# Accumulating attention scores of successive key tiles in one PSUM bank per head, instead of starting a bank for every key tile

## The chip, the cores and the metric

The kernel runs on one core of a Trainium2 chip. The metric is the device time of one execution in microseconds. The engines are named as in the profile: PE (TensorE's matmuls), PEld (its weight loads), DVE (VectorE), ACT (ScalarE), POOL (GpSimd), SP (SyncE, which issues the transfers). Matmul results land in PSUM, which has eight banks of 128 partitions by 512 fp32 values.

## The reference

A transformer layer of attention and a mixture of experts, both fed with the same normalised input; everything is fp32. Attention has 4 sequences of 2048 tokens, width 512, 16 heads of 32.

```python
xn = _layernorm(x, axis=-1)
# attention
qkv = jnp.einsum('bnc,dc->bnd', xn, qkv_w) + qkv_b
q, k, v = ...
attn = jnp.einsum('bhqd,bhkd->bhqk', q, k) * HEAD_DIM ** (-0.5)
attn = jax.nn.softmax(attn, axis=-1)
out = jnp.einsum('bhqk,bhkd->bhqd', attn, v)
a = jnp.einsum('bnc,dc->bnd', out, proj_w) + proj_b
# experts: the first token of a sequence chooses two of eight for the whole sequence
_, idx = jax.lax.top_k(xn[:, 0, :] @ Wr + br, 2)
h = jax.nn.gelu(jnp.einsum('bsd,bkde->bkse', xn, W1[idx]) + b1[idx], approximate=False)
o = jnp.einsum('bkse,bkef->bksf', h, W2[idx]) + b2[idx]
return x + a + jnp.sum(o, axis=1) / 2
```

## The kernel before

**Units.** Attention is cut into 1024 units. The order is: 4 sequences, 4 groups of 4 heads (GH = 4, 32 rows of the array for each head), 4 chunks of 512 queries (CH), 16 tiles of 128 keys (NT). The number of a unit is U, its key tile kt. The loop over U starts 22 units early (LEAD), since each unit also does the first pass of the unit that lies 22 ahead: the maxima of the scores. A chunk's softmax is computed in two passes. The first pass (`score_max`, L526) computes scores with queries on the partitions, 128 queries by 512 keys per head, and DVE reduces each bank to a column of negated maxima (L662). At the end of a chunk the maxima are split into three bf16 parts (`split`), transposed (`turn_maxima`) and kept as `negm`.

**The second pass of a unit**, with keys on the partitions: `shift` (L536) starts a bank for each of the 4 heads with minus the maximum of every query, a bf16 matmul of `ones_b` and `negm`; `score` (L544) adds the scores of 128 keys by 512 queries onto it; ACT takes the exponential from the bank into the tile `p` (L656, 4 instructions a unit, one per head). `weigh` (L556) multiplies p with v in every even unit, for the two units before, into one bank `acc`, which DVE adds to `sacc` (L565, or L562 for the first of a chunk). POOL adds the p of a chunk up to `psum` (L573, L575), one addition of 128x2048 for each key tile but the first; `add_keys` (L581) sums those over the keys.

**The order in a unit** is written out by hand (`manual_schedule`): the four shifts, then scores of heads 0 and 1, maxima of heads 2 and 3, scores of heads 2 and 3, maxima of heads 0 and 1 (so that four matmuls use the four row groups at once); then the exps, a Gelu where one is due, the four reduces, reciprocals and the attention's division, POOL's addition, in even units `weigh`, and last, in most odd units, one item of other work: a projection to q, k or v, a quarter of an expert layer or of the output projection (`dense`, L395, tiles kps, qps, vps, hps, ops, prps), 16 matmuls of 128x32 tiles. Its bank is emptied by DVE or ACT. A planner (`Plan`) places these items in the odd units; 38 odd units remain without one, most of them at kt = 13.

**PSUM.** All of it is one pool of 8 banks taken in turn (`ps`, bufs=8), by `s`, `m`, `acc`, the projections, transposes and key sums alike. A bank's new tile waits for the engine that read the old one. A unit with an `acc` or a projection takes nine banks: s0 to s3, m2, m3, m0, m1, then the ninth.

**SBUF.** `p` has 4 buffers of 8 KB a partition. `kT` holds the keys of a group as 4 tiles of 512 (2 groups at a time), `qT` the queries.

Of the kernel before, what the change touches and what calls it, by code (L numbers as in the profile page):

```python
# [9 lines left out]
F32 = mybir.dt.float32  # L10
BF16 = mybir.dt.bfloat16
U32 = mybir.dt.uint32
AF = mybir.ActivationFunctionType
ALU = mybir.AluOpType
# [3 lines left out]
P = 128  # L18
HEADS = 16
HD = 32  # L20
GH = P // HD
TOP_K = 2
EPS = 1e-5
CH = 512


AHEAD = 6
WARN = 4


class Plan:
# [6 lines left out]
    def __init__(self, B, DC, NCH, NT, TPC):  # L38
        self.per_group = NCH * NT
        self.per_seq = DC * self.per_group  # L40
        self.units = B * self.per_seq
        self.lead = NT + AHEAD
        self.items = {}
# [43 lines left out]
        for b in range(B):  # L87
            t0 = slots[0] if b == 0 else self.first_load[("xf", (b, 0))] + WARN
            for c in range(NCH):
# [4 lines left out]
        for b in range(B):  # L94
            for qc in range(NCH):
# [3 lines left out]
                self.first_load[("xl", ("at", b, qc))] = done + 1  # L99
                proj.append((done + 1 + WARN, [("proj", b, qc, i) for i in range(TPC)]))  # L100

# [64 lines left out]
    def loads(self, bufs, start):  # L166
# [3 lines left out]
        for s, tag, key in self.uses:  # L170
            tiles = live.setdefault(tag, [])
            if key not in [t[0] for t in tiles]:
                free = start
                if len(tiles) == bufs[tag]:
                    free = tiles.pop(0)[1]
                at = max(free, s - 2 * WARN, start, self.first_load.get((tag, key), start))
                assert at < s, (s, tag, key, at, free)
# [9 lines left out]
def block_kernel(  # L187
# [16 lines left out]
    nc = tc.nc  # L204
    B, N, D = x.shape
    E = Wr.shape[1]
    DC = D // P
    NT = N // P
    NCH = N // CH
    TPC = CH // P  # L210
    SCALE = float(HD) ** -0.5
    PSUM = bass.MemoryType.PSUM
    plan = Plan(B, DC, NCH, NT, TPC)
# [2 lines left out]
    ctx.enter_context(tc.manual_schedule())  # L216
    const = ctx.enter_context(tc.tile_pool(name="const", bufs=1))
    kv_pool = ctx.enter_context(tc.tile_pool(name="kv", bufs=2 * NCH))
    p_pool = ctx.enter_context(tc.tile_pool(name="p", bufs=4))
    pair = ctx.enter_context(tc.tile_pool(name="pair", bufs=2))  # L220
    stream = ctx.enter_context(tc.tile_pool(name="stream", bufs=1))
    small = ctx.enter_context(tc.tile_pool(name="small", bufs=2))
    ps = ctx.enter_context(tc.tile_pool(name="ps", bufs=8, space=PSUM))

    def bank(name):
        return ps.tile([P, CH], F32, tag="bank", name=name)

    def rows_of(j):
        return slice(j * HD, (j + 1) * HD)


    xn_dram, v_dram, att_dram, part_dram = {}, {}, {}, {}
# [70 lines left out]
    ones_b = const.tile([P, P], BF16, name="ones_b")  # L303
# [4 lines left out]
    for i in range(2):  # L308
        t = const.tile([P, TPC, GH, HD], BF16, name=f"spread{i}")
# [6 lines left out]
    for c, tag in enumerate(("xl", "xf", "h", "h")):  # L316
        t = stream.tile([P, TPC, D], F32, tag=tag, name=f"x_0_{c}", bufs=2 if tag == "h" else 1)
# [79 lines left out]
                    start=(first and n == 0), stop=(last and n == len(terms) - 1),  # L397
                )

    kT, qT = {}, {}  # L400
    hT, bias, b1s = {}, {}, {}

    def with_bias(dst, src, col, on_dve):
# [102 lines left out]
    def place(u):  # L506
        rest, kt = divmod(u, NT)
        rest, qc = divmod(rest, NCH)
        return (*divmod(rest, DC), qc, kt)

    mx, negm, sacc, psums, sums, pT = {}, {}, {}, {}, {}, {}
    curves, waiting, ends = {}, {}, []

    def later(u, do):
        waiting.setdefault(u, []).append(do)
# [12 lines left out]
            )  # L528
            tiles.append((mx[b, g, qc][:, j, i, kc : kc + 1], t))

    def shift(u, heads, tiles):
        b, g, qc, kt = place(u)
        for j in heads:
            tiles[j] = bank(f"s{j}_{u}")
            r = rows_of(j)
            nc.tensor.matmul(  # L536
                tiles[j], ones_b[r, :], negm[b, g, qc][r, :], start=True, stop=False
            )

    def score(u, heads, tiles):  # L540
        b, g, qc, kt = place(u)
        for j in heads:
            r = rows_of(j)
            nc.tensor.matmul(  # L544
                tiles[j], kT[b, g, kt // TPC][r, ts(kt % TPC, P)], qT[b, g, qc][r, :],
                start=False, stop=True,
            )

    def weigh(u):

# [74 lines left out]
    def divide(where):  # L625
        att[where] = pair.tile([P, CH], F32, tag="att", name="att_%d_%d_%d" % where)
        nc.gpsimd.tensor_tensor(att[where], sacc[where], sums[where], ALU.mult)
# [8 lines left out]
    for U in range(-LEAD, plan.units):  # L636
        second = U >= 0
        first_pass = U + LEAD if U + LEAD < plan.units else None
        chunk, kt = divmod(U, NT)
        b, g, qc, _ = place(U) if second else (0, 0, 0, 0)  # L640
        maxima, tiles = [], {}


        if second:
            shift(U, range(GH), tiles)
        for h in range(2):
            if second:
                score(U, (2 * h, 2 * h + 1), tiles)
            if first_pass is not None:
                score_max(first_pass, (2 - 2 * h, 3 - 2 * h), maxima)  # L650


        if second:
            pT[U] = p_pool.tile([P, GH, CH], F32, tag="p", name=f"p_{U}")
            for j in range(GH):
                nc.scalar.activation(pT[U][:, j, :], tiles[j], AF.Exp, scale=SCALE)  # L656
        curve = curves.pop(U, None)
        if curve is not None:
            flat = curve.rearrange("p f n -> p (f n)")
            nc.scalar.activation(flat, flat, AF.Gelu)  # L660
        for dst, t in maxima:
            nc.vector.tensor_reduce(dst, t, AX.X, ALU.max, negate=True)  # L662
        last = U + LEAD
        if first_pass is not None and last % NT == NT - 1:
            where, n = place(last)[:3], last // NT
            rest = split(where, n)
            mark = U
            pending = (rest, where, n, mark)
        if last % NT == 0 and 0 < last <= plan.units:
            pending[0]()  # L670
        before = place(U - NT)[:3] if U >= NT else None
        if before is not None and kt in (5, 7, 9, 11):
            q = ts((kt - 5) // 2, P)
            nc.vector.reciprocal(sums[before][:, q], sums[before][:, q])  # L674
        if before is not None and kt == 12:
            divide(before)
            later(U + 2, lambda w=before: nc.sync.dma_start(
                att_dram[w[0], w[2]][:, w[1], :], att[w]))
        for t, key in row_ready.pop(U, []):
            nc.gpsimd.tensor_tensor(t, t, bias[key[0]], ALU.add)  # L680
        if second:
            add_weights(U)


        if second and U % 2 == 0:
            if U >= 2:
                weigh(U - 2)
            if U - 2 >= plan.units - NT:
                add_last(U - 2)
            if kt == 4 and before is not None:  # L690
                add_keys(before, bank("keys_%d_%d_%d" % before), [psums[before]], False)
        for step, sb, n in plan.extra.get(U, []):
            if step == "stats":
                if n == 0:
                    norms[sb] = stat_tiles(sb)
                stats(norms[sb][0], n, held["xl", ("stats", sb, n // TPC)][:, n % TPC, :])
            elif step == "root":
                root(*norms[sb], 0, NT)
            elif step == "normal":
                normal(held["xl", ("normal", sb, n // TPC)][:, n % TPC, :], *norms[sb][1:], n)  # L700
            else:
                c, i = divmod(n, TPC)
                xs = held["xq", ("stage", sb, c)]
                turn(xs, held["xl", ("normal", sb, c)][:, i, :], i, f"{sb}_{n}")
                if i == TPC - 1:
                    later(U + 1, lambda sb=sb, c=c, xs=xs: nc.sync.dma_start(xn_dram[sb, c], xs))
        if last % NT == 3 and NT < last <= plan.units + 3:
            turn_maxima(*pending[1:3])
        for item in plan.items.get(U, []):
            dense(item, U, curve is not None)  # L710


        for do in waiting.pop(U, []):
            do()
        for s, tag, key in loads.get(U, []):
            t = load(tag, key)
            if tag == "row":
                row_ready.setdefault(U + 4, []).append((t, key))
        if g == 2 and qc == 0 and kt == 0 and second and b + 1 < B:
            new_bias = load_bias(b + 1)  # L720
        if g == 2 and qc == 0 and kt == 5 and second and b + 1 < B:
            sum_bias(*new_bias)

        for n, c in ((16, NCH - 1), (1, NCH - 2)):
            if U == plan.units - n:
                tags = ("xf", "xq") if c == NCH - 1 else ("xl", "xq")
                t, rows = (
                    stream.tile([P, TPC, D], F32, tag=tag, name=f"end_{tag}", bufs=BUFS[tag])
                    for tag in tags
                )  # L730
                for i in range(TPC):
                    nc.sync.dma_start(rows[:, i, :], part_dram[B - 1, c, i])
                n = DC - 1 if c == NCH - 1 else DC
                nc.sync.dma_start(t[:, :n, :], att_dram[B - 1, c][:, :n, :])
                ends += [t, rows]


    U = plan.units
    weigh(U - 2)
    add_last(U - 2)  # L740
    where = place(U - 1)[:3]
# [69 lines left out]
```

## Time and profile before

| | |
|---|---|
| median of 3 runs | 5135.53 us (5134.29 to 5135.7) |
| the profiled execution | 5133.48 us, its span 5131.6 us |
| TensorE's granted clock | 0.998 |
| first shift, last shift | 160.1 us, 5085.2 us |
| L662, 4096 maxima on DVE | 2542.9 us busy, 683 ns each |
| L656, 4096 exps on ACT | 2118.1 us busy, 602 ns each |
| L544, 4096 scores, and L526, 4096 maxima, on PE | 1924.0 and 1908.4 us busy, side by side |
| L395, six kinds of projections on PE | 1806 us busy in all |

An fp32 matmul is two records in the profile, one for each pass over the moving operand; 8192 records are 4096 matmuls. The matmuls of the four row groups (or column groups) run side by side, so the busy time of a group is the union of its records and a record's mean length is not what it adds. The matmul's own ends are modelled; the intervals between starts are the better measure. The line "idle before, releaser" says how long an engine stood still just before a group's instructions and who let it go on. In the timeline the columns are start, length, engine, line, operation, tiles, and the idle time before it.

### The profile page before, as it was taken

The numbers are of one execution on the slowest core, as the hardware profiler recorded it, in microseconds if no ns is written. First come the engines' busy times: TensorE is split into PE (matmuls) and PEld (weight loads), VectorE is DVE, ScalarE is ACT, GpSimd is POOL, SyncE is SP. The second block draws the span as 40 slices with busy tenths as digits, with TensorE's granted clock in tenths as the row PEclk, the third lists the DMA queues.
The fourth block names the chain that finished last, engine by engine and source line by source line (L and its number), as shares of the span: only waits on it lengthen the run. The fifth ranks groups of instructions, "written<-read, shape, count | busy, mean of one in ns | idle before, by whom it ended". The sixth has DMA issues, their size and how long they took to land.

```text
span 5131.6 us, 108175 instructions
## 1 busy us (share of the span) xinstructions
PE 5054.0 (98%) x46020; PEld 1776.4 (35%) x46020; DVE 3449.0 (67%) x5495; ACT 2516.2 (49%) x4571; POOL 4534.6 (88%) x1430
## 2 busy tenths in 40 slices
PE   8999999999999999999999999999999999999998
PEld 2333333333333333333333333333333333333333
DVE  5666676766766667666766767766667666666672
ACT  1455545554544545554445454555444454555543
POOL 0699898989999999999999999989999999999992
PEclk9999999999999999999999999999999999999999
DMA  4211112201122112221121221221112211021112
GB/s 165 69 62 51 46 65 89 102 30 38 67 85 69 65 65 80 72 81 44 48 93 46 79 85 54 85 85 59 40 56 89 78 63 59 18 75 34 40 43 78
DMA packets 220675, 340.20 MB, mean 66 GB/s; under 512 B 14364, under 2 KB 129052, under 8 KB 205984
## 3 DMA queue, kind: packets, MB, share of 16 engines
q1 hardware_dynamic: 220192, 333.28, 19.2%
q8 instruction: 361, 5.91, 0.5%
q14 instruction: 122, 1.00, 0.1%
HBM read 249.61 MB, written 83.62 MB: 65 GB/s over the span
## 4 chain that ended last, share of the span: by engine, by line
PE 95%; POOL 2%; ACT 1%; DVE 0%; issue 0%; DMA 0%; SPq 0%; ACTq 0%; POOLq 0%
PE acc L556 18%; PE m L526 17%; PE s L544 17%; PE ops L395 9%; PE hps L395 9%; PE s L536 7%; PE kps L395 4%; PE vps L395 4%; PE qps L395 4%; PE prps L395 4%; POOL psum L575 2%; PE keys L581 1%; ACT L656 1%; PE xt L365 1%; ACT p L656 1%; PE mt L618 0%
## 5 line engine op out<-in xcount | busy, mean ns | idle before, releaser
L575 POOL TENSOR_TENSOR psum<-psum,p 128x2048 f32<-128x2048 f32 x882 | 4008.6, 4545 | 217.3 <-ACT p L656 182.1
L662 DVE TENSOR_REDUCE mx<-m 128x1 f32<-128x512 f32 x4096 | 2542.9, 683 | 1057.5 <-PE m L526 1056.9
L656 ACT ACTIVATE p<-s 128x512 f32<-128x512 f32 x4096 | 2118.1, 602 | 1797.3 <-PE m L526 1717.9
L544 PE MATMUL s<-qT,kT 32*128 32x512 f32 x8192 | 1924.0, 589 | 0.0
L526 PE MATMUL m<-kT,qT 32*128 32x512 f32 x8192 | 1908.4, 590 | 2.7 <-DMA wk<-in_qkv_wT_dram 1.5
L526 PEld LDWEIGHTS m<-kT,qT 32*128 32x128 f32 x8192 | 929.1, 184 | 325.3 <-issue 242.3
L556 PE MATMUL acc<-p,v 128*32 128x512 f32 x8192 | 990.0, 599 | 38.5 <-ACT p L656 38.5
L544 PEld LDWEIGHTS s<-qT,kT 32*128 32x128 f32 x8192 | 765.6, 186 | 31.0 <-issue 12.8
L556 PEld LDWEIGHTS acc<-p,v 128*32 128x32 f32 x8192 | 215.3, 109 | 738.5 <-ACT p L656 428.6
L395 PE MATMUL hps<-xf,w 128*32 128x512 f32 x4096 | 466.0, 595 | 0.2 <-ACT p L656 0.2
L395 PE MATMUL ops<-wb_w,h 128*32 128x512 f32 x4096 | 466.0, 595 | 0.2 <-ACT p L656 0.2
L536 PE MATMUL s<-negm,ones_b 32*128 32x512 bf16 x4096 | 421.4, 385 | 5.3 <-ACT p L656 3.5
L565 DVE TENSOR_TENSOR sacc<-acc,sacc 128x512 f32<-128x512 f32 x448 | 309.9, 692 | 154.7 <-PE acc L556 154.7
L536 PEld LDWEIGHTS <-ones_b 32*128 32x128 bf16 x4096 | 108.6, 91 | 842.3 <-issue 835.2
L573 POOL TENSOR_TENSOR psum<-p,p 128x2048 f32<-128x2048 f32 x63 | 286.1, 4541 | 117.6 <-ACT p L656 117.6
L407 ACT ACTIVATE h<-hps,b 128x512 f32<-128x512 f32 x115 | 79.0, 687 | 353.6 <-PE hps L395 353.6
L674 DVE RECIPROCAL sums<-sums 128x128 f32<-128x128 f32 x252 | 237.3, 942 | 0.7 <-ACT sums L593 0.7
L395 PE MATMUL vps<-wb_v,xq 128*32 128x512 f32 x2048 | 233.0, 595 | 2.3 <-issue 2.0
L395 PEld LDWEIGHTS ops<-wb_w,h 128*32 128x32 f32 x4096 | 120.0, 109 | 317.6 <-issue 229.8
L395 PEld LDWEIGHTS hps<-xf,w 128*32 128x32 f32 x4096 | 120.0, 109 | 317.1 <-issue 232.1
L395 PE MATMUL kps<-xq,wk 128*32 128x512 f32 x1920 | 218.4, 595 | 1.0 <-ACT p L656 0.2
L395 PE MATMUL qps<-xq,wq 128*32 128x512 f32 x1920 | 218.4, 595 | 0.1
(89 smaller groups left out, 1710.8 us busy)
## 6 DMA issues: line engine op xcount, KB each, us to landing
xq<-xn_dram SPq DMA_DIRECT2D x64, 1024.0 KB, 5.7
w<-in_W_dram SPq DMA_DIRECT2D x128, 256.0 KB, 3.1
xn_dram<-xq_stage SPq DMA_DIRECT2D x16, 1024.0 KB, 7.1
v_dram<-v SPq DMA_DIRECT2D x64, 256.0 KB, 2.4
xf<-xn_dram SPq DMA_DIRECT2D x16, 1024.0 KB, 6.1
v<-v_dram SPq DMA_DIRECT2D x64, 256.0 KB, 4.0
row<-in_x_dram SPq DMA_DIRECT2D x64, 256.0 KB, 5.9
part_dram<-row SPq DMA_DIRECT2D x64, 256.0 KB, 2.1
```

The source lines that it names most:

```text
L395: nc.tensor.matmul(pp[rows_of(j), :], lhsT[:, rows_of(j)], rhs, start=(first and n == 0), stop=(last and n == len(terms) - 1),)
L407: nc.scalar.activation(dst, src, AF.Identity, bias=col)
L526: nc.tensor.matmul(t, qT[b, g, qc][r, ts(i, P)], kT[b, g, kc][r, :], start=True, stop=True)
L536: nc.tensor.matmul(tiles[j], ones_b[r, :], negm[b, g, qc][r, :], start=True, stop=False)
L544: nc.tensor.matmul(tiles[j], kT[b, g, kt // TPC][r, ts(kt % TPC, P)], qT[b, g, qc][r, :], start=False, stop=True,)
L556: nc.tensor.matmul(acc[r, :], held["v", (b, g, kt // TPC)][:, (kt + n) % TPC, r], pT[u + n][:, j, :], start=(n == 0), stop=(n == 1),)
L565: nc.vector.tensor_tensor(t, acc, t, ALU.add)
L573: nc.gpsimd.tensor_tensor(psums[b, g, qc], pT[u - 1], pT[u], ALU.add)
L575: nc.gpsimd.tensor_tensor(psums[b, g, qc], psums[b, g, qc], pT[u], ALU.add)
L656: nc.scalar.activation(pT[U][:, j, :], tiles[j], AF.Exp, scale=SCALE)
L662: nc.vector.tensor_reduce(dst, t, AX.X, ALU.max, negate=True)
L674: nc.vector.reciprocal(sums[before][:, q], sums[before][:, q])
```

## The change

One bank per head (`s_bank`) now belongs to the scores for the whole kernel. The shift is put in once at the start of a chunk. The scores of the first key tile are added onto it, and each following key tile adds q times the *difference* between its keys and those of the tile before (`kD`), so that the bank holds, after each unit, the shifted scores of that unit's keys. The exp reads the bank between two such additions.

- `shift` runs in 64 units instead of 1024.
- `differences` makes `kD` on DVE: for each group and each of its 4 key tiles of 512, one subtraction of 384 columns and, but for the first tile, one of 128. They stand behind the reduces in the units with kt = 7, 11 and 15 before a group and kt = 3 in it.
- The rotating pool `ps` has 4 banks instead of 8, for `m`, `acc`, the projections, transposes and key sums.
- `p` has 3 buffers instead of 4; the room goes to `kD` (4 tiles of 2 KB a partition).

```diff
+DIFF = 55
...
-    p_pool = ctx.enter_context(tc.tile_pool(name="p", bufs=4))
+    p_pool = ctx.enter_context(tc.tile_pool(name="p", bufs=3))
...
-    ps = ctx.enter_context(tc.tile_pool(name="ps", bufs=8, space=PSUM))
+    ps = ctx.enter_context(tc.tile_pool(name="ps", bufs=4, space=PSUM))
+    s_pool = ctx.enter_context(tc.tile_pool(name="s", bufs=1, space=PSUM))
...
+    s_bank = [s_pool.tile([P, CH], F32, tag=f"s{j}", name=f"s{j}") for j in range(GH)]
...
-    def shift(u, heads, tiles):
-        b, g, qc, kt = place(u)
-        for j in heads:
-            tiles[j] = bank(f"s{j}_{u}")
-            r = rows_of(j)
-            nc.tensor.matmul(
-                tiles[j], ones_b[r, :], negm[b, g, qc][r, :], start=True, stop=False
-            )
+    def shift(where):
+        for j in range(GH):
+            r = rows_of(j)
+            nc.tensor.matmul(s_bank[j], ones_b[r, :], negm[where][r, :], start=True, stop=True)
 
-    def score(u, heads, tiles):
+    def score(u, heads):
         b, g, qc, kt = place(u)
+        k = (kD if kt else kT)[b, g, kt // TPC]
         for j in heads:
             r = rows_of(j)
             nc.tensor.matmul(
-                tiles[j], kT[b, g, kt // TPC][r, ts(kt % TPC, P)], qT[b, g, qc][r, :],
-                start=False, stop=True,
+                s_bank[j], k[r, ts(kt % TPC, P)], qT[b, g, qc][r, :],
+                start=False, stop=True, skip_group_check=True,
             )
+
+    def differences(b, g, c):
+
+        t = kD[b, g, c] = kv_pool.tile([P, CH], F32, tag="kd", name=f"kD_{b}_{g}_{c}", bufs=NCH)
+        k = kT[b, g, c]
+        nc.vector.tensor_tensor(t[:, P:], k[:, P:], k[:, : CH - P], ALU.subtract)
+        if c:
+            nc.vector.tensor_tensor(t[:, :P], k[:, :P], kT[b, g, c - 1][:, CH - P :], ALU.subtract)
...
-        if second:
-            shift(U, range(GH), tiles)
+        if second and kt == 0:
+            shift((b, g, qc))
...
-                score(U, (2 * h, 2 * h + 1), tiles)
+                score(U, (2 * h, 2 * h + 1))
...
-                nc.scalar.activation(pT[U][:, j, :], tiles[j], AF.Exp, scale=SCALE)
+                nc.scalar.activation(pT[U][:, j, :], s_bank[j], AF.Exp, scale=SCALE)
...
+        G, n = divmod(U + plan.per_group - DIFF, plan.per_group)
+        if n % TPC == 0 and n // TPC < NCH and G < B * DC:
+            differences(*divmod(G, DC), n // TPC)
```

More of the change, by code (lines that the diff above doesn't have):

```diff
@@ L398, in product @@
                 )
-    kT, qT = {}, {}
+    kT, qT, kD = {}, {}, {}
     hT, bias, b1s = {}, {}, {}
@@ L640, in block_kernel @@
         b, g, qc, _ = place(U) if second else (0, 0, 0, 0)
-        maxima, tiles = [], {}
-        if second:
-            shift(U, range(GH), tiles)
+        maxima = []
+        if second and kt == 0:
+            shift((b, g, qc))
         for h in range(2):
             if second:
-                score(U, (2 * h, 2 * h + 1), tiles)
+                score(U, (2 * h, 2 * h + 1))
             if first_pass is not None:
```

## The prediction

> **What bounds the kernel now.** I read the busy shares first, then the chain that ended last, then the groups, and last the timeline of single units, since a share says nothing about which wait ends a unit.
>
> ```profile
> PE 5054.0 (98%) x46020; PEld 1776.4 (35%) x46020; DVE 3449.0 (67%) x5495; ACT 2516.2 (49%) x4571; POOL 4534.6 (88%) x1430
> ...
> PE 95%; POOL 2%; ACT 1%; DVE 0%; issue 0%; DMA 0%; SPq 0%; ACTq 0%; POOLq 0%
> ...
> L575 POOL TENSOR_TENSOR psum<-psum,p 128x2048 f32<-128x2048 f32 x882 | 4008.6, 4545 | 217.3 <-ACT p L656 182.1
> ...
> L556 PE MATMUL acc<-p,v 128*32 128x512 f32 x8192 | 990.0, 599 | 38.5 <-ACT p L656 38.5
> ...
> L536 PE MATMUL s<-negm,ones_b 32*128 32x512 bf16 x4096 | 421.4, 385 | 5.3 <-ACT p L656 3.5
> ```
>
> TensorE (PE) carries 95% of the chain and is almost never idle; POOL is next with 88%. The group to be removed, L536, is busy for 421 us, and the tempting forecast takes 15/16 of that. The timeline of one unit says otherwise:
>
> ```profile
> 2503.83 0.39 PE L536 MATMUL s<-negm,ones_b 32*128 32x512 bf16 x4
> ...
> 2504.06 0.59 PE L544 MATMUL s<-qT,kT 32*128 32x512 f32 x2
> ...
> 2505.17 2.07 ACT L656 ACTIVATE p<-s 128x512 f32<-128x512 f32 x4 [3.55 <-PE m L526]
> 2505.20 2.48 DVE L662 TENSOR_REDUCE mx<-m 128x1 f32<-128x512 f32 x4 [0.54 <-PE m L526]
> ...
> 2505.88 1.92 PE L556 MATMUL acc<-p,v 128*32 128x512 f32 x16
> ...
> 2507.73 0.39 PE L536 MATMUL s<-negm,ones_b 32*128 32x512 bf16 x4
> ```
>
> What to see: the shift's 0.39 us overlap the scores, which start 0.23 us after it. An even unit lasts 3.90 us (2503.83 to 2507.73); an odd one with a projection 5.61 us by the same reading. Call a unit's start T: scores at T+0.23, weighing at T+2.04. The second pass of the first maximum's matmul ends at T+1.25, DVE begins its reduce 0.12 later, at T+1.37, and a single reduce takes 0.69.
>
> **Removed: the shift in 960 of 1024 units.** By intervals that is 960 x 0.23 = 220 us. [...] the scores (32x128 tiles) would now follow the 128x32 work directly and pay what the small bf16 shift covered. The lead-in units, which have maxima but no shift, show that price:
>
> ```profile
> 104.11 0.31 PEld L526 LDWEIGHTS m<-kT,qT 32*128 32x128 f32 x8 [0.84 <-DVE mx L662]
> 104.11 1.14 PE L526 MATMUL m<-kT,qT 32*128 32x512 f32 x8
> 105.18 0.16 PEld L395 LDWEIGHTS vps<-wb_v,xq 128*32 128x32 f32 x8 [0.76 <-DVE mx L662]
> 105.18 0.64 PE L395 MATMUL vps<-wb_v,xq 128*32 128x512 f32 x4
> ```
>
> The single records in these rows have the first fp32 pass take 0.535 us to the next one (104.11 to 104.65) where passes behind a shift take 0.43. So 0.11 of the 0.23 comes back as a weight load that nothing hides. Four passes then put the last one at 0.535 + 2 x 0.43 = T+1.39, and the change of mode another 0.535 later: weighing could start at T+1.93. [...] the shift is worth 0.11 us a unit, not 0.23.
>
> **Added: a new wait, the bank.** This is where I expect the rest to go. Before, banks rotated over 8 with nine taken in most units: the weighing's (or projection's) bank had been s0's, free when the first exp ended (2505.17 + 0.60 = 2505.77, T+1.94), ahead of T+2.04. Afterwards the four rotating banks serve m2, m3, m0, m1 and then acc or a projection: the fifth takes the bank of m2 **of the same unit**, and the instruction order has it wait for DVE's first reduce. That ends: second pass of m2 starts at T+0.55, ends T+1.14, reduce T+1.25 to T+1.94; a release by DVE reaches a weight load 0.05 us later in this trace (evacuation ends 2504.66, load 2504.71). So weighing starts at T+2.00: after T+1.93, before the old T+2.04. An ordinary unit saves 0.047 us. Behind the wait on PE stand this unit's 8 or 16 matmuls and the next unit's scores; everyone waits for those. The bound from below is no bubble (saves 0.114), from above a release 0.05 later, as for example 0.10 in all (saves nothing).
>
> The last maximum (m1) of a unit takes the bank of the previous acc or projection, as before; its load waits until T+0.88 now and would be wanted in the pass starting at T+0.97. Unhidden it costs 0.11, so 0.02 late, which the bank wait covers; if the whole 0.18 us of the load counted, weighing would slip to T+2.02.
>
> About 883 units of the 943 whose weighing or projection starts at T+2.04 are not at a chunk's start: 883 x 0.047 = **-41.5 us**. The 60 others keep the shift and still take the bank wait (T+0.23+1.88 = 2.11): **+4.5 us**.
>
> **A stall that goes.** L556's 38.5 us of idling on ACT are 35 waits of up to 1.2 us in units after a Gelu, whose table loads delay the exps and so s0's bank:
>
> ```profile
> 192.17 1.92 PE L556 MATMUL acc<-p,v 128*32 128x512 f32 x16 [1.16 <-ACT p L656]
> ```
>
> 31 units start the weighing at T+3.27. With m2's bank it starts at T+2.00. What is late next: the next unit's third and fourth score need the late exps, which end about T+4.7, and would be wanted near T+4.4 with the pass at T+4.8. I take 0.1 off: 31 x (1.27 - 0.1) = **-36 us**.
>
> **Single score buffers.** Scores of a unit wait for the exp of the same head in the unit before. In an even unit the exps end by T+3.3, the next scores start at T+3.85: hidden. Uncovered only in about 32 odd units without a projection; there the old order waited for all four exps, the new one waits on m3's and m0's reduces instead. Worked through, those pairs gain 0.06 us (27 with a transpose of maxima) to 0.5 us (5): **-4 us**. In 35 units the maxima's transpose is followed by a projection, whose bank is m3's: reduce ends T+2.54, load T+2.60, wanted T+2.44: 35 x 0.16 = **+6 us**.
>
> **p from 4 to 3 buffers.** An exp then waits for POOL's addition three units back. Laying the additions' ends beside the exps' starts in the trace, this would have bitten in 8 units, all behind unit 990 where projections run out and POOL already sets the pace; POOL's end lets go one unit later, about one addition (4.5 us). With the small PE gains lost there: **+7 us**. Elsewhere POOL idles about 5 us in each chunk of 75 to 79 us.
>
> **Differences.** 64 of 384 and 48 of 128 columns on DVE, about 0.56 us and 0.29 us (292 ns is the row of the SBUF addition at L760, an estimate for the wide one from that and a 512-wide 692 ns): 50 us in all. They stand in odd units behind the reduces (end T+3.7) and end before the projection's evacuation at T+5.7, with a reciprocal (0.94) too: 5.6. Without that cover they cost at most their 50 us. [...] by the rows (4545 ns, alike beside every DVE group) nothing. I take 0.
>
> **Sum:** -41.5 + 4.5 - 36 - 4 + 6 + 7 = -64 us against 5133.5 us of the profiled execution (span 5131.6): 5069. The median of the runs is 2 us higher, which I leave inside the range.
>
> **Rivals.**
> - *No bubble* (bank free by T+1.93): 883 x 0.114 + 31 x 1.34 less 4 net elsewhere = 139, **4995**. For it: only 0.07 us separates them. Against: the reduce's start 0.12 after the pass is the same in 967 units. Chance 0.15.
> - *All eaten*: m1's load counts in full, or the bank's release takes 0.10: saves 0 to 0.023 a unit, **5090 to 5110**. Chance 0.17.
> - *The interval saved whole*[...]: 220 us, **4913** (POOL, 4635 us of additions and small work from 167 us on plus the tail, allows 4880). The lead-in speaks against. Chance 0.03.
> - *Slower: the reduce becomes the clock.* Every delay of DVE's first reduce now stops PE in the same unit, 943 times; before, its bank was wanted a unit later. From 0.07 us beyond my T+2.00 it eats everything; at 0.10 it gives **5163**. For it: in 35 units the first reduce starts 0.7 to 2 us late. Against: DVE's evacuation ends near T+0.9, 0.35 before the reduce can start. Chance 0.09.
> - The forecast itself: 0.56.
>
> The range 4990 to 5115 takes in the first two rivals; 4913 and 5163 stay out with 0.12. Faster by over 0.2% (below 5125; a smaller difference can't be told from none here): forecast, no bubble, whole interval and most of the eaten case, 0.84; within 0.2%: 0.06; slower: 0.10.
>
> **What would show it.** Ordinary units of 3.85 and 5.57 us between starts of scores, with acc's weight load idling on "DVE mx", not on ACT; L536 down to 256 matmuls; the 1.2 us waits behind Gelu gone; the first score pass 0.1 us longer. Units of 3.79 would mean no bubble; 3.9 or more, that the bank wait ate it. Long ACT waits on POOL in all chunks would mean that I misjudged the three p buffers.

## The result, and the profile after

The changed kernel takes **5358.87 us** (median of 6 runs, 5355.02 to 5362.38) against 5134.91 us: a ratio of 1.0436, 95% interval 1.0423 to 1.0449. It is slower by 224 us where 5069 was forecast. The profiled execution took 5355.02 us, its span 5353.2 us, at a mean granted clock of 0.978 (0.998 before).

The page of the changed kernel, the lines that answer to those shown of before, and from the groups by line the two subtractions:

```profile
PE 5155.7 (96%) x42180; PEld 1671.0 (31%) x42180; DVE 3740.7 (70%) x5607; ACT 2518.2 (47%) x4571; POOL 4549.6 (85%) x1430
...
PE 88%; DVE 9%; POOL 1%; issue 1%; DMA 0%; ACT 0%; SPq 0%; DVEq 0%; POOLq 0%
...
L586 POOL TENSOR_TENSOR psum<-psum,p 128x2048 f32<-128x2048 f32 x882 | 4020.7, 4559 | 282.7 <-ACT p L667 246.3
```

```profile
L558 DVE TENSOR_TENSOR kD<-kT,kT 128x128 f32<-128x128 f32 x48 | 183.9, 3831 | 0.0
L556 DVE TENSOR_TENSOR kD<-kT 128x384 f32<-128x384 f32 x64 | 119.4, 1865 | 0.0
```

PE's 95% of the chain are down to 88%, and DVE, which was nowhere on it, holds 9%. The small groups say why: 128 columns take 3831 ns on average, more than five times as long as a reduce of 512 columns (683 ns), and twice as long as the subtraction of 384 columns just in front. The two lines are busy for 303 us where I had put 50. A mean that doesn't follow the size speaks for a wait inside the instruction.

What the ordinary unit does is as it was worked out. Timeline of the changed kernel, DVE's and PE's rows of one odd unit:

```profile
2602.81 0.70 PE L547 MATMUL s<-qT,kD 32*128 32x512 f32 x2
...
2604.06 2.48 DVE L673 TENSOR_REDUCE mx<-m 128x1 f32<-128x512 f32 x4 [0.41 <-PE m L532]
...
2604.80 3.64 PE L401 MATMUL vps<-wb_v,xq 128*32 128x512 f32 x32
2608.38 0.40 PE L540 MATMUL s<-negm,ones_b 32*128 32x512 bf16 x4
```

With T = 2602.81 the reduce starts at T+1.25, the projection at T+1.99 and the next unit at T+5.57. The first score pass is 0.70 us long, 0.59 once the loads are hidden.

What went wrong stands at the end of a group. Timeline of the changed kernel from 485 us on, DVE's, POOL's and PE's rows:

```profile
485.50 2.48 DVE L673 TENSOR_REDUCE mx<-m 128x1 f32<-128x512 f32 x4 [0.41 <-PE m L532]
487.90 2.35 DVE L556 TENSOR_TENSOR kD<-kT 128x384 f32<-128x384 f32 x1
490.17 4.58 DVE L558 TENSOR_TENSOR kD<-kT,kT 128x128 f32<-128x128 f32 x1
494.68 0.68 DVE L456 SCALAR_TENSOR_TENSOR row<-ops,row 128x512 f32<-128x512 f32 x1
495.28 1.87 DVE L673 TENSOR_REDUCE mx<-m 128x1 f32<-128x512 f32 x3
```

```profile
485.28 4.56 POOL L586 TENSOR_TENSOR psum<-psum,p 128x2048 f32<-128x2048 f32 x1
489.92 4.69 POOL L586 TENSOR_TENSOR psum<-psum,p 128x2048 f32<-128x2048 f32 x1
```

```profile
491.34 0.59 PE L547 MATMUL s<-qT,kT 32*128 32x512 f32 x2
495.42 2.07 PE L532 MATMUL m<-kT,qT 32*128 32x512 f32 x2 [3.49 <-DVE row L456]
497.41 3.64 PE L567 MATMUL acc<-p,v 128*32 128x512 f32 x16
```

Put the ends side by side. POOL's addition ends at 489.84; the first subtraction, issued at 487.90, ends 0.41 later. POOL's next addition is on record from 489.92 and ends at 494.61; the second subtraction, issued at 490.17, ends 0.14 later, at 494.75. Beside no addition the same two take 0.55 and 0.28 us. So DVE doesn't share with POOL here, it stands until the addition is through.

The other subtractions in the trace fit: of the 112, seven run beside nothing on POOL and take those 0.55 or 0.28 us. The other 105 end a fixed time after an instruction of POOL, 0.41 to 0.42 us with 384 columns and 0.14 to 0.15 us with 128; in six of them that instruction is not an addition of `p` but the shorter one of the bias to `row` (L694, 128x512), and these six took only 1.35 to 1.38 us.

Behind the pair in DVE's order stands the emptying of the projection's bank (L456), and one of the four rotating banks is then what PE's next maximum needs: PE stops for 3.49 us. Its matmuls after that are slow (3.64 us for the weighing in place of 1.92), since the clock is halved there. Windows of the changed kernel, each with its length, busy times and the granted clock behind POOL's busy time:

```profile
482.20:489.00 6.80, 6.80 (x62) 2.16 (x64) 5.76 (x9) 2.90 (x6) 6.72 (x2) 1.00 0.22 65
489.00:506.10 17.10, 13.61 (x92) 3.80 (x84) 12.02 (x12) 4.13 (x8) 7.02 (x3) 0.80 0.00 1
```

The clock's records know only 1 and 0.5, so a mean of 0.80 over 17.1 us is half the clock for 6.8 of them. Laying unit by unit against before, the 221.6 us between the spans are 21.5 in the lead-in and 200.3 up to the start of the last unit. Of the latter, 68 units stretched by over 0.5 us add 277, and all others give back 77. Of the 277, 245 fall on 43 units with the numbers 60, 0 and 4 in a group of 64, each just behind a unit with a pair of subtractions (59, 63 and 3). Of the other 25, eleven lie behind number 990, ten of which are stretched in the run without subtractions (below) as well.

### The profile page after: what moved, and what is told of

Same layout as the page of the kernel before. It is cut to its first block, busy times and chain, and to the rows that moved or that the text cites. A ratio compares the mean times of both kernels' runs of the same rounds, so it can differ in the third digit from the quotient of the medians.

```text
span 5353.2 us, 100529 instructions
## 1 busy us (share of the span) xinstructions
PE 5155.7 (96%) x42180; PEld 1671.0 (31%) x42180; DVE 3740.7 (70%) x5607; ACT 2518.2 (47%) x4571; POOL 4549.6 (85%) x1430
## 4 chain that ended last, share of the span: by engine, by line
PE 88%; DVE 9%; POOL 1%; issue 1%; DMA 0%; ACT 0%; SPq 0%; DVEq 0%; POOLq 0%
PE s L547 19%; PE acc L567 19%; PE m L532 16%; PE ops L401 8%; PE hps L401 8%; PE qps L401 4%; PE kps L401 4%; PE vps L401 4%; DVE mx L673 3%; PE prps L401 3%; DVE kD L558 3%; DVE kD L556 2%; PE keys L592 1%; POOL psum L586 1%; PE xt L371 1%
## 5 line engine op out<-in xcount | busy, mean ns | idle before, releaser
L586 POOL TENSOR_TENSOR psum<-psum,p 128x2048 f32<-128x2048 f32 x882 | 4020.7, 4559 | 282.7 <-ACT p L667 246.3
L532 PE MATMUL m<-kT,qT 32*128 32x512 f32 x8192 | 2126.4, 621 | 98.6 <-DVE row L456 45.1
L547 PE MATMUL s<-qT,kD 32*128 32x512 f32 x7680 | 1943.7, 617 | 8.0 <-ACT p L667 7.8
L567 PE MATMUL acc<-p,v 128*32 128x512 f32 x8192 | 1049.8, 632 | 52.6 <-DVE mx L673 52.6
L532 PEld LDWEIGHTS m<-kT,qT 32*128 32x128 f32 x8192 | 826.8, 185 | 524.7 <-issue 240.9
L547 PEld LDWEIGHTS s<-qT,kD 32*128 32x128 f32 x7680 | 673.4, 185 | 833.6 <-issue 487.7
L584 POOL TENSOR_TENSOR psum<-p,p 128x2048 f32<-128x2048 f32 x63 | 286.4, 4545 | 213.1 <-ACT p L667 213.1
L401 PE MATMUL prps<-wb_proj,xl_at 128*32 128x512 f32 x1792 | 203.9, 595 | 0.0
L456 DVE SCALAR_TENSOR_TENSOR row<-ops,row 128x512 f32<-128x512 f32 x128 | 87.7, 685 | 146.7 <-PE ops L401 110.6
```

Source lines behind the costliest of these rows:

```text
L401: nc.tensor.matmul(pp[rows_of(j), :], lhsT[:, rows_of(j)], rhs, start=(first and n == 0), stop=(last and n == len(terms) - 1),)
L532: nc.tensor.matmul(t, qT[b, g, qc][r, ts(i, P)], kT[b, g, kc][r, :], start=True, stop=True)
L547: nc.tensor.matmul(s_bank[j], k[r, ts(kt % TPC, P)], qT[b, g, qc][r, :], start=False, stop=True, skip_group_check=True,)
L567: nc.tensor.matmul(acc[r, :], held["v", (b, g, kt // TPC)][:, (kt + n) % TPC, r], pT[u + n][:, j, :], start=(n == 0), stop=(n == 1),)
L584: nc.gpsimd.tensor_tensor(psums[b, g, qc], pT[u - 1], pT[u], ALU.add)
L586: nc.gpsimd.tensor_tensor(psums[b, g, qc], psums[b, g, qc], pT[u], ALU.add)
```

## The experiments

The theory after this reading: **DVE's subtraction is shut out while POOL adds, what stands behind it on DVE is late, and with four rotating banks PE stops at once.** Rivals: the split of PSUM itself, the three p buffers, and a mere sharing of bandwidth between DVE and POOL.

**Without the subtractions.** Scores of each key tile are added in full, so the output is no attention; the exp's scale keeps it finite.

```diff
-        k = (kD if kt else kT)[b, g, kt // TPC]
+        k = kT[b, g, kt // TPC]
...
-                nc.scalar.activation(pT[U][:, j, :], s_bank[j], AF.Exp, scale=SCALE)
+                nc.scalar.activation(pT[U][:, j, :], s_bank[j], AF.Exp, scale=1e-4)
...
-            differences(*divmod(G, DC), n // TPC)
+            pass
```

> The differences are left out (the scores of each key tile are added in full, with the exp's scale small enough to stay finite, so the values are not attention's); matmuls, waits and banks are those of the changed kernel. Theory (a DVE subtraction with two SBUF operands waits until POOL's addition in flight has ended, and everything behind it on DVE waits too): the 68 stretched units and the half-clock stretches go, the saving in ordinary units (some 77 us) and the slower lead-in (some 21 us) stay: 5065 to 5095 us. Rival (four rotating banks and single score banks are what costs): stays above 5250 us.

Measured 5086.58 us, ratio 0.9905 (0.9888 to 0.9921), clock 0.997. All the same matmuls, banks and buffers: 272 us of the changed kernel hang on 112 small DVE instructions. The rival of the banks falls, and with it that of the three p buffers, which this run has too.

**The subtractions on POOL**, the whole change with DVE kept out of them.

```diff
-        nc.vector.tensor_tensor(t[:, P:], k[:, P:], k[:, : CH - P], ALU.subtract)
+        nc.gpsimd.tensor_tensor(t[:, P:], k[:, P:], k[:, : CH - P], ALU.subtract)
...
-            nc.vector.tensor_tensor(t[:, :P], k[:, :P], kT[b, g, c - 1][:, CH - P :], ALU.subtract)
+            nc.gpsimd.tensor_tensor(t[:, :P], k[:, :P], kT[b, g, c - 1][:, CH - P :], ALU.subtract)
```

> The same subtractions, but on POOL. Theory: DVE is free of them, POOL carries some 1.3 us for each of 64 pairs, mostly in its idle time: 5075 to 5115 us. Rival (banks): above 5250 us. Rival (three p buffers leave POOL no room): 5150 to 5250 us, with ACT waiting for POOL around the ends of groups.

Measured 5100.25 us, ratio 0.9931 (0.9914 to 0.9947). On POOL each takes its own time and no more (groups of this run by line):

```profile
L556 POOL TENSOR_TENSOR kD<-kT 128x384 f32<-128x384 f32 x64 | 64.7, 1011 | 0.0
L558 POOL TENSOR_TENSOR kD<-kT,kT 128x128 f32<-128x128 f32 x48 | 22.3, 464 | 0.0
```

87 us more on an engine that is 88% busy cost 14 us of time.

**Four columns.** The subtractions stay on DVE, cut to 4 columns (scores and exp as in the run without them).

```diff
-        nc.vector.tensor_tensor(t[:, P:], k[:, P:], k[:, : CH - P], ALU.subtract)
+        nc.vector.tensor_tensor(t[:, P : P + 4], k[:, P : P + 4], k[:, :4], ALU.subtract)
...
-            nc.vector.tensor_tensor(t[:, :P], k[:, :P], kT[b, g, c - 1][:, CH - P :], ALU.subtract)
+            nc.vector.tensor_tensor(t[:, :4], k[:, :4], kT[b, g, c - 1][:, CH - P : CH - P + 4], ALU.subtract)
```

> The subtractions on DVE cut to 4 columns each (scores added in full with a small exp scale, as in the run without differences). Theory (exclusion: the instruction can't start its work while POOL adds): each still lasts up to 4.6 us and the time stays at 5280 to 5355 us. Rival (the two share bandwidth, so that the cost goes with the columns): below 5100 us.

Measured 5131.71 us, ratio 0.9992 (0.9983 to 1.0002): in neither range, 45 us above the run without subtractions. The groups by line tell what happened:

```profile
L556 DVE TENSOR_TENSOR kD<-kT 128x4 f32<-128x4 f32 x64 | 109.8, 1715 | 0.0
L558 DVE TENSOR_TENSOR kD<-kT,kT 128x4 f32<-128x4 f32 x48 | 7.2, 149 | 0.0
```

The first of a pair still takes 1715 ns for four columns, almost what 384 took, and up to 4.46 us: all 61 that met an addition end 0.02 to 0.03 us after its end. Bandwidth can't be it. But the second takes 149 ns: the first is done so early that the second gets in before POOL's next addition. In the changed kernel the first runs on for 0.41 us, POOL's next addition takes its turn, and the second waits a whole addition. That the second is caught only for that reason I had not thought of; it makes most of DVE's lost time (183.9 of 303 us).

**One SBUF operand.** A multiplication by a constant in place of each subtraction (scores and exp again as in the run without them).

```diff
-        nc.vector.tensor_tensor(t[:, P:], k[:, P:], k[:, : CH - P], ALU.subtract)
+        nc.vector.tensor_scalar(t[:, P:], k[:, P:], 0.5, None, ALU.mult)
...
-            nc.vector.tensor_tensor(t[:, :P], k[:, :P], kT[b, g, c - 1][:, CH - P :], ALU.subtract)
+            nc.vector.tensor_scalar(t[:, :P], k[:, :P], 0.5, None, ALU.mult)
```

> In place of each subtraction a DVE multiplication by a constant of the same size, with one SBUF operand (scores added in full with a small exp scale). If any fp32 DVE instruction between SBUF and SBUF is shut out by POOL's addition, as the 3061 ns of a 16-column addition of a constant in the kernel before suggests: 5250 to 5355 us. If two SBUF operands are needed for it: 5065 to 5100 us.

Measured 5340.69 us, ratio 1.0399 (1.0378 to 1.042), and the lengths are like those of the subtractions:

```profile
L558 DVE TENSOR_SCALAR kD<-kT 128x128 f32<-128x128 f32 x48 | 185.3, 3860 | 0.0
L556 DVE TENSOR_SCALAR kD<-kT 128x384 f32<-128x384 f32 x64 | 101.9, 1592 | 0.0
```

Two SBUF operands aren't needed for the wait.

**The pair apart.** Both on DVE in full size, the second two units later.

```diff
-        if c:
-            nc.vector.tensor_tensor(t[:, :P], k[:, :P], kT[b, g, c - 1][:, CH - P :], ALU.subtract)
+
+    def seam(b, g, c):
+        t, k = kD[b, g, c], kT[b, g, c]
+        nc.vector.tensor_tensor(t[:, :P], k[:, :P], kT[b, g, c - 1][:, CH - P :], ALU.subtract)
...
+        if n % TPC == 2 and 0 < n // TPC < NCH and G < B * DC:
+            seam(*divmod(G, DC), n // TPC)
```

> The changed kernel with the 128-column subtraction two units after the 384-column one, both on DVE. Theory (a DVE subtraction waits for the addition in flight, and the second of a pair is caught by the next addition because POOL takes its turn as soon as the first is done): each waits part of one addition only, some 2 us on average, no pair blocks DVE for a whole 4.6 us and more, and most of PE's stops go: 5140 to 5210 us, with the 128-column ones spread between 0.3 and 4.6 us. Rival (any such subtraction takes a whole addition): the 128-column ones stay at 4.6 us, above 5280 us.

Measured 5282.34 us, ratio 1.0288 (1.0271 to 1.0305): my range was missed, and the rival's time was met. The lengths fit the exclusion all the same, not a fixed price: the 48 small ones take 0.28 to 4.52 us. What I had wrong is the average, 3.4 us in place of some 2. In units where POOL isn't behind, its addition starts as soon as the fourth exp is done, just ahead of the end of DVE's fourth reduce, so that the subtraction meets a fresh addition: 31 of the 48 take 4.27 us or more. DVE's and POOL's rows of this run:

```profile
497.77 4.40 DVE L560 TENSOR_TENSOR kD<-kT,kT 128x128 f32<-128x128 f32 x1
502.10 0.68 DVE L456 SCALAR_TENSOR_TENSOR row<-ops,row 128x512 f32<-128x512 f32 x1
```

```profile
497.48 4.54 POOL L586 TENSOR_TENSOR psum<-p,p 128x2048 f32<-128x2048 f32 x1 [2.52 <-ACT p L669]
```

POOL starts 0.29 us before DVE and ends at 502.02; DVE ends at 502.17. In all, the subtractions hold DVE for longer here than in the changed kernel (328 us against 303), and yet the time is 77 us shorter: each block is about one addition long at most, and PE stands still for over 3 us once, against 27 times.

**The split of PSUM alone.** The kernel before, with a shift in every unit, but one fixed bank per head for the scores and four that rotate.

```diff
-    ps = ctx.enter_context(tc.tile_pool(name="ps", bufs=8, space=PSUM))
+    ps = ctx.enter_context(tc.tile_pool(name="ps", bufs=4, space=PSUM))
+    s_pool = ctx.enter_context(tc.tile_pool(name="s", bufs=1, space=PSUM))
...
-            tiles[j] = bank(f"s{j}_{u}")
+            tiles[j] = s_pool.tile([P, CH], F32, tag=f"s{j}", name=f"s{j}_{u}")
```

> The kernel before (a shift in every unit, no differences), with PSUM split as in the change: one fixed bank per head for the scores and four rotating ones. Theory of the prediction (weighing waits for the first reduce of its own unit, 0.07 us later than before when the shift stays; the waits behind Gelu go, 36 us; the lead-in costs 19): 5165 to 5215 us. Rival (the banks cost nothing that shows): 5125 to 5145 us.

Measured 5216.12 us, ratio 1.0158 (1.0143 to 1.0174), 1 us above the range. Its ordinary units last 0.07 us longer than before, as forecast, and its lead-in 24 us more. Of the 31 units behind a Gelu, 25 last 0.88 us less, but the unit after each of these 0.46 us or more longer; so the gain there is smaller than the 36 us that were put in. The bank wait is real and of the size forecast in an ordinary unit.

**Three p buffers alone.** The kernel before with `bufs=3` for `p`.

> The kernel before with three p buffers in place of four, nothing else. Prediction's step: about one addition later at the end, 5134 to 5146 us. Rival (POOL's lag bites in every chunk): above 5160 us.

Measured 5139.46 us, ratio 1.0008 (1.0 to 1.0017): 4 us more, inside the range.

**A better version.** The subtractions on POOL, and the maxima of the lead-in units in the score banks, which stand idle there:

```diff
-            t = bank(f"m{j}_{u}")
+            t = bank(f"m{j}_{u}") if u >= LEAD else s_bank[j]
```

> Subtractions on POOL, and the maxima of the 22 lead-in units use the four score banks, which stand idle there, so that each lead-in unit's maximum no longer waits for the emptying of the projection before it. Theory (the lead-in's units went from 4.64 to 5.50 us for that wait): some 20 us below the 5100 us of the run with subtractions on POOL, 5072 to 5088 us. Rival (something else in the lead-in, as the stores of v): 5095 to 5102 us.

Measured **5080.26 us**, ratio 0.9891 (0.9876 to 0.9906): the lead-in's 20 us come back, and this beats both kernels.

**Another place for the subtractions on POOL.** On top of that, the first tile's in the last unit before a group and the other three in its first.

```diff
-        G, n = divmod(U + plan.per_group - DIFF, plan.per_group)
-        if n % TPC == 0 and n // TPC < NCH and G < B * DC:
-            differences(*divmod(G, DC), n // TPC)
+        G, n = divmod(U + 1, plan.per_group)
+        if n < 2 and G < B * DC:
+            for c in (range(1, NCH) if n else (0,)):
+                differences(*divmod(G, DC), c)
```

> As g1_lead, with the subtractions moved to the last unit before a group (the first tile) and the first unit of it (the other three), where POOL has no addition. If the 14 us between subtractions on POOL and none at all come from POOL running late in a group's last chunk: 5062 to 5078 us. If they come from something else: as g1_lead, within 5 us.

Measured 5094.82 us, ratio 0.9919 (0.9905 to 0.9932): 15 us slower than the version before, and in neither range. This run has waits of PE for the subtractions that the version before doesn't have:

```profile
PEld s L547 <- POOL kD L556: 24.3, 11, 4.3
PE s L547 <- POOL kD L556: 14.6, 7, 3.4
```

POOL comes to the first tile's subtraction behind its additions, and the scores of the group's second unit wait for it. What the 14 us between POOL and no subtractions are made of stays open; of the 15.5 us between the spans of the two profiled executions, 4.7 lie ahead of the first score.

## Why the prediction was wrong

Direction and size failed on **one term: "by the rows (4545 ns, alike beside every DVE group) nothing. I take 0"**, with "without that cover they cost at most their 50 us". The subtractions cost 272 us (5358.87 less 5086.58). The step failed twice. The 50 us came from an SBUF addition of 292 ns at L760, which runs in the tail, where POOL adds nothing; it is no price beside an addition. And POOL's steady 4545 ns were read as proof of no conflict. But of the 3130 us that DVE works beside those additions in the trace of before, 2858 go to instructions that read PSUM, and the reduces among them show no wait: the 2932 of L662 that lie wholly inside an addition take 681 ns in the median, as those beside none do. Nor need the cost fall on POOL: in the changed kernel POOL's additions (L584 and L586) took 12 us more in all than before, while the subtractions held DVE for 303. What was measured is that DVE stands until POOL is through: 105 of the 112 subtractions end 0.14 to 0.42 us after an instruction of POOL.

The trace of before held the row. DVE and POOL there, where the variances are made ready for their root:

```profile
783.42 4.28 DVE L343 TENSOR_SCALAR sd<-mv 128x16 f32<-128x16 f32 x1
```

```profile
783.14 4.53 POOL L573 TENSOR_TENSOR psum<-p,p 128x2048 f32<-128x2048 f32 x1 [1.02 <-ACT p L656]
```

Sixteen columns in 4.28 us, ended 0.03 after POOL's addition. The line has three such instructions in mid-kernel, of 4.28, 0.61 and 4.30 us, and each ended 0.03 us after an addition. Four of the same line ahead of POOL's additions (of 4 columns) took 0.17 us. At such a price a pair would have come to as much as 9 us.

How 303 us of DVE become 272 of time can be read from PE's busy time, which the page of the run without subtractions gives as

```profile
PE 5033.5 (99%) x42180; PEld 1651.0 (32%) x42180; DVE 3447.0 (68%) x5495; ACT 2518.3 (50%) x4571; POOL 4536.5 (89%) x1430
```

The spans are 5353.2 and 5083.7 us. Of these 269.5 us between them, PE stands still for 147 (197.5 idle in the changed kernel, 50.2 without subtractions) and is busy for the other 122, with the same 42180 matmul records. Most of the 122 is laid to the halved clock: the clock records of the trace have half the clock for 242 us against 33, and PE is busy in 203 and 25 of these. Half of the difference, 89 us, is an estimate of what the slow clock cost. In the changed kernel 42 of the 43 stretches at half the clock begin some 2 to 5 us after the start of a stop of PE of 1.5 to 5.8 us; 23 of them last 6.8 us, 18 last 3.4. In the run with the pair apart stops of 1.1 to 2.5 us lie ahead of 31 such stretches (mean clock 0.986). Why a stop of PE is followed by half the clock is not shown.

Point by point, the rest:

- **The shift**: held. Not 0.23 us a unit, since 0.11 comes back as an unhidden load; the first pass is 0.535 us to the next, as in the lead-in.
- **The bank wait**: held. Ordinary units save 0.054 us (0.047 forecast), those at a chunk's start lose 0.067 (0.075).
- **Gelu**: held, 1.27 us in each such unit (1.17 after a deduction that did not come); a table load ahead of the exps takes 1.28 us in both traces.
- **Maxima's transpose before a projection**: +0.107 us (0.16 less 0.047 = 0.11 forecast).
- **p buffers**: +4 us alone (+7 forecast with PE's lost gains).
- **Left out**: the lead-in. Its units went from 4.64 to 5.50 us, since all four maxima form a single round there and the last waits for the previous projection's bank; I had looked at that wait only where it is hidden. 21.5 us.

Forecast and lead-in make 5069 + 21.5 = 5090.5, against 5086.6 measured without the subtractions; their 272 us are the rest. The rival "the reduce becomes the clock" had the right chain (late DVE, then the bank, then PE) and the wrong cause: it charged every unit a tenth of a microsecond instead of a few units many.

## What to carry to other kernels

Before giving DVE an instruction whose operands and result all lie in SBUF, ask what POOL is running at that moment and for how long: the price can be POOL's whole instruction (here up to 4.62 us for 128 columns that take 0.28 alone), and POOL's own row hardly shows it (4559 ns in place of 4545). Look for an instruction of DVE with few columns and a long mean; it can mark such a wait. And when buffers are cut, check who stands behind the slowest instruction of the engine that empties them: here, by the waits in the trace, a pool of four banks turned DVE's late evacuation into PE's stop (3.49 us in the stretch shown), and half the clock followed the stop (6.8 us). No run had the subtractions on DVE with more rotating banks, so how much of the loss more banks would have saved is not shown.

## What was not expected of the hardware

- The subtractions and multiplications of DVE (fp32, from SBUF to SBUF) end a fixed time after the instruction of POOL in flight, however long before that they were issued. Behind POOL's addition of p it was 0.14 us for a subtraction of 128 columns, 0.41 for one of 384, and 0.02 for one of 4; for a multiplication by a constant it was 0.08 (128 columns) and 0.22 (384).
- POOL waits as well. In the changed kernel, 50 additions of p that start on record while a subtraction of 384 columns has some 0.34 us left last 4.69 to 4.75 us (4.55 in the median of the others), and nine additions of the bias to `row` that start in the same way 1.59 to 1.61 us (1.29 in the median). So POOL loses 0.1 to 0.3 us at a time.
- Who comes next depends on tenths of a microsecond: the second of a pair of 4 columns got through between two additions (149 ns), the second of a pair of 384 and 128 waited some 4.6 us in 38 of 48 cases.
- The reciprocal (128 columns, SBUF to SBUF) is not shut out: 937 to 953 ns before and after, although 141 of the 252 in the changed kernel lie wholly inside an instruction of POOL. Why it differs wasn't tried.
